# A second level of the seven-product identity in the last block's wide product, and a bias carried as a row of the adapters

## The chip, the cores and the metric

The kernel runs on one core of a Trainium2 chip. The metric is the device time of an execution in microseconds: 261.69 us, the median of three runs (261.42 to 261.91). A core has five engines that run side by side[...]: TensorE (PE: matmuls; PEld: their weight loads), VectorE (DVE), ScalarE (ACT), GpSimd (POOL) and SyncE (SP), whose queue issues nearly all transfers here. Matmuls write into PSUM banks[...].

## The reference, cut to what matters

```python
q_emb = relu(cond @ W3 + b3)                      # (64, 512)
v_sum = sum(v, axis=1, keepdims=True)             # v: (64, 64, 512)
y = relu(((64 * v + v_sum) * q_emb[:, None]) @ W2 + b2)
base = y @ W_base + b_base                        # 512 x 512
shared = (y @ A_s) @ B_s                          # rank 16
gates = softmax(y @ W_router + b_router)          # 6 experts, top 2 kept
routed = sum over e of ((y @ A_r[e]) * w[e]) @ B_r[e]
out = v + base + shared + routed
```

So there are two wide products of 512 by 512 for 4096 tokens, the first with `W2`, the second with `W_base`, all in float32, and between them the gate: the small product `y @ [A_s, A_r, W_router]`, a softmax over six experts, and the two largest kept.

## The kernel before

Everything is held transposed: features on the partitions, tokens along the columns. The tokens go through in four blocks (k = 0 to 3) of 1024, and a block is two column halves (h) of 512. With four chunks of 128 features, a block of y or x is a tile of 128 x (4 chunks, 2 halves, 512).

Both wide products use the seven-product identity of Strassen in Winograd's form. The weight is cut in four quarters of 256 by 256, the block likewise (two feature halves by two column halves); `weight_sums` and `row_sums` build four sums on each side, and seven quarter products (numbered 1 to 7) replace eight. The four row sums in their order are a21 + a22 (the factor of product 5), that minus a11 (of 6), a11 - a21 (of 7), and a12 minus the second (of 3); the factors of 1, 2 and 4 are a11, a12 and a22 themselves. A quarter product is four matmuls of 512 columns (two chunks of depth, two of output). In blocks 1 to 3 the first product applies the identity a second time, inside each of the seven (`first_inner`): each quarter product becomes seven matmuls of 128 x 128 x 256 columns, `q(n, t)`, with n the inner product and t the place in an outer order. The inner products of one t share two banks, "a" and "b", each of two halves (`lo`, `hi`). Between them ScalarE copies a partial result from one half to another (`seed_y`, `seed_z`), and VectorE adds finished parts to the results (`take_1`, `take_21`, `take_22`, `take_u`, `take_w5`; ScalarE copies where nothing is to be added). There are six such banks, so the banks of t come free for t + 3 when the takes of t are done.

The inner identity needs its own sums of sums. For the weights `inner_weight_sums` builds them once (`inner_t`, from `w2_sb` and `t2`, on VectorE). For the rows `prepare_inner` builds them: most on VectorE ahead of time, those of products 2 and 4 on GpSimd inside `first_inner` (L315 to L318: eight subtractions and additions of 256 columns), followed on GpSimd by the e3 and p5 adds (L543, L546), which combine two results, and then ScalarE's bias and relu (L340) into y.

The loop of a block (L758 on): `first_inner` (block 0: `first_mixed`), the loads of the x rows that are added at the end (`load_rows`, into four tiles that the first product has just left), eight groups of small matmuls into `ph` (L779), with the last part of the first product (`rest`) after the second group, the row sums of y on VectorE (L263 to L266), and `second`, which has the gate.

`gate` is a chain of twelve small operations on VectorE with ScalarE's exp among them. Then `hw` weighs the adapters' activations (L683, VectorE), eight transposes turn it round (L704, into `pt`), ScalarE copies it to `hwT`, and GpSimd takes the difference of the two halves, `hwd` (L708). The adapters' second weights `bcat_sb` (112 rows: seven adapters of rank 16) enter as eight more matmuls into the same banks (L641). A result leaves as `with_x` (L637: bank + bias column `bb_sb` + x row, on VectorE) or `leave` (L662), followed by its store. In block 3 the last bank is cut into 384 and 128 columns (`last`, `part`, `last_routed`), whose stores go by two queues, so that the one that ends last is small.

While `second` runs, the preparation of the next block's rows is dealt out in portions (`behind`, `fill`, `share`): the sums over tokens of `modulate` (L206 to L208: scale q, reduce, multiply by q, on VectorE), ScalarE's scaling (L212), the row sums and inner sums. What a portion has not done by then `first_inner` does. All four engines keep the order in which the code issues their instructions; nothing reorders it.

Of the kernel before, what the change touches and what calls it, by code (L numbers as in the profile page):

```python
# [9 lines left out]
F32 = mybir.dt.float32  # L10
AF = mybir.ActivationFunctionType
ALU = mybir.AluOpType
# [20 lines left out]
HC = GR + E  # L33


@with_exitstack
def adaln_ffn(ctx: ExitStack, tc: tile.TileContext, xa, x0, x1, head, w3, w2, wb, a, bcat, br, outT):
# [47 lines left out]
    NH0 = NQ * B + 3 * NC  # L85
    head_sb = const.tile([P, NH0 + NQ * P], F32, tag="head_sb", name="head_sb")
    cond_sb = head_sb[:, : NQ * B].rearrange("p (c b) -> p c b", c=NQ)
    b3_sb, b2_sb, bb_sb = (head_sb[:, NQ * B + n * NC : NQ * B + (n + 1) * NC] for n in range(3))
# [30 lines left out]
    bcat_sb = loaded(bcat, [GR, D], "bcat_sb")  # L119
# [24 lines left out]
    def inner_weight_sums(w, t, name):  # L144

        at = {i: n for n, i in enumerate((5, 6, 7, 4, 1, 2, 3))}
        it = const.tile([P, 4, 7, P], F32, tag=name, name=name)
# [10 lines left out]
        for o, b in groups:  # L158
            i = [it[:, n, o] for n in range(4)]
            steps += [  # L160
                lambda i=i, b=b: nc.vector.tensor_tensor(i[0], b(0, 1), b(0, 0), ALU.subtract),
                lambda i=i, b=b: nc.vector.tensor_tensor(i[1], b(1, 1), i[0], ALU.subtract),
                lambda i=i, b=b: nc.vector.tensor_tensor(i[2], b(1, 1), b(0, 1), ALU.subtract),
                lambda i=i, b=b: nc.vector.tensor_tensor(i[3], b(1, 0), i[1], ALU.subtract),
            ]
# [89 lines left out]
    def row_sums(a, name, cols=slice(0, TB)):  # L255
# [5 lines left out]
        def steps(c=slice(0, KH)):  # L261
# [4 lines left out]
                lambda: nc.vector.tensor_tensor(s[3][:, c], a12[:, c], s[1][:, c], ALU.subtract),  # L266
# [31 lines left out]

    def prepare_inner(k):
# [13 lines left out]
        def steps(g, a, engine=nc.vector):  # L313
            return [
                lambda: engine.tensor_tensor(s[g][:, 0], a(0, 1), a(1, 1), ALU.add),  # L315
                lambda: engine.tensor_tensor(s[g][:, 1], s[g][:, 0], a(0, 0), ALU.subtract),
                lambda: engine.tensor_tensor(s[g][:, 2], a(0, 0), a(0, 1), ALU.subtract),
                lambda: engine.tensor_tensor(s[g][:, 3], a(1, 0), s[g][:, 1], ALU.subtract),  # L318
            ]

# [103 lines left out]
    def first_inner(k, y):  # L424
# [94 lines left out]
        for step in inner[k]["late"]:  # L519
            step()  # L520
        fill(2)
# [52 lines left out]
    def gate(k, ph):  # L574
# [10 lines left out]
        nc.scalar.activation(g, lg, AF.Exp)  # L585
        sm = small.tile([P, 2 * NS], F32, tag="sm", name=f"sm_{k}")
# [29 lines left out]
    def second(k, y, ph, res):  # L616
# [17 lines left out]
        def with_x(name, j, f, h):  # L634

            t = row(f, h)
            nc.vector.scalar_tensor_tensor(t, ps[name, j], bb_sb[:, f : f + 1], t, ALU.add, ALU.add)  # L637
            return t
# [9 lines left out]
        def part(p, cols, i, start):  # L648
            for c in range(KH):
                nc.tensor.matmul(  # L650
                    p[:, cols], tb[i][:, c, ts(1, P)], sy[i][:, c, cols], start=start and c == 0, stop=False,
                    skip_group_check=True,
                )

        def last_routed(p, cols, hw):
            nc.tensor.matmul(
                p[:, cols], bcat_sb[:, ts(KH + 1, P)], hw[:GR, cols], start=False, stop=True,
                skip_group_check=True,
            )

        def leave(p, f, h, add, cols=slice(0, TB), queue=nc.sync):
            nc.vector.tensor_tensor(add[:, cols], p[:, cols], add[:, cols], ALU.add)  # L662
            queue.dma_start(outT[k, f, h, :, cols], add[:, cols])
# [5 lines left out]
        def share():  # L669
# [12 lines left out]
        hw = small.tile([P, 2 * NS, GR], F32, tag="hw", name=f"hw_{k}")  # L682
        nc.vector.tensor_tensor(  # L683
            hw.rearrange("p s (g r) -> p s g r", r=R),
            ph[:, :, :GR].rearrange("p s (g r) -> p s g r", r=R),
            w.unsqueeze(3).to_broadcast([P, 2 * NS, G, R]),
            ALU.mult,
        )
# [12 lines left out]
        pt = ps_h.tile([P, 2 * NS, P], F32, tag="ph", name=f"pt_{k}")  # L701
        hwT = small.tile([P, 2, TB], F32, tag="hwT", name=f"hwT_{k}")
        for s in range(2 * NS):
            nc.tensor.transpose(pt[:GR, s, :], hw[:, s, :], ident)  # L704
        for h in range(2):
            nc.scalar.copy(hwT[:GR, h], pt[:GR, ts(h, NS)].rearrange("p s t -> p (s t)"))  # L706
        hwd = small.tile([P, TB], F32, tag="hwd", name=f"hwd_{k}")
        nc.gpsimd.tensor_tensor(hwd[:GR], hwT[:GR, 0], hwT[:GR, 1], ALU.subtract)  # L708
# [4 lines left out]
        routed("x", 0, 0, hwT[:GR, 0])  # L713
        finish("x", 0, 0, 0)
        routed("z", 0, 0, hwT[:GR, 1])
        finish("z", 0, 0, 1)

        routed("w", 0, KH, hwT[:GR, 1])
        leave(ps["w", 0], KH, 1, u22[0])
        share()  # L720
        if k < NB - 1:
            prod(5, 1, "w")
            routed("w", 1, KH + 1, hwT[:GR, 1])
            leave(ps["w", 1], KH + 1, 1, u22[1])
        else:
            last = [(ps_p.tile([P, TB], F32, tag="pp", name=f"last_{lo}"), slice(lo, hi), queue)
                    for lo, hi, queue in ((0, 3 * P, nc.sync), (3 * P, TB, nc.scalar))]
            for p, cols, queue in last:
                part(p, cols, 5, True)
                last_routed(p, cols, hwT[:, 1])  # L730
                leave(p, KH + 1, 1, u22[1], cols, queue)
# [106 lines left out]
```

## Time and profile before

| | us |
|---|---|
| median of three runs (range) | 261.69 (261.42 to 261.91) |
| the profiled execution | 261.56 |
| its span, first to last instruction | 259.8 |
| TensorE busy | 254.8 (98%) |
| VectorE busy | 193.9 (75%) |
| ScalarE busy | 136.5 (53%) |
| GpSimd busy | 38.7 (15%) |
| block 3: first product | 196.0 to 217.1, and 0.4 after the second group |
| block 3: eight groups of small matmuls | 217.1 to 224.7 |
| block 3: second product with adapters | 224.7 to 256.6 |

The profile gives one execution in us from its first instruction. A row of a timeline has start, duration, engine, line, operation, output <- inputs, sizes, how many are merged, and in brackets the idle time before it and what ended it. In the chain a row is start, duration and what then held up the end. PE's rows count instructions: a float32 matmul is two.

### The profile page before, as it was taken

What the parts mean: (1) busy time and instruction counts of PE and PEld (TensorE: products, weight loads), DVE (VectorE), ACT (ScalarE), POOL (GpSimd) and SP (SyncE); (2) the same over time, 40 slices, a digit from 0 to 9 for tenths busy, and PEclk for the clock granted to TensorE, in tenths of its full rate; (3) what the DMA queues carried; (4) which work ended last, traced back from release to release, by engine and by line L of the source; (5) the groups of instructions that cost most, each with busy time, mean ns of one, the idle gap of its engine ahead of it and who ended that gap; (6) DMA issues with size and microseconds to landing.
All of it is one profiled execution on the core that took longest, in us unless ns stands there. A gap on an engine that the chain in (4) does not pass through costs nothing.

```text
span 259.8 us, 3177 instructions
## 1 busy us (share of the span) xinstructions
PE 254.8 (98%) x1004; PEld 164.5 (63%) x1004; DVE 193.9 (75%) x386; ACT 136.5 (53%) x373; POOL 38.7 (15%) x53
## 2 busy tenths in 40 slices
PE   7999999999999999999999999999999999999995
PEld 3756896454478888444458889544447889745453
DVE  2899898799968967968995894988895475872332
ACT  2399496596048896289017889349404428112000
POOL 1000000020017610002006630002001770000100
PEclk9999999999999999999999999999999999999999
DMA  6997629303320044000521025200332023400233
GB/s 194 360 352 295 261 99 390 156 3 121 121 81 0 11 156 161 0 3 6 196 81 42 0 83 168 76 0 3 121 121 81 0 77 92 159 0 3 76 139 108
DMA packets 14145, 28.54 MB, mean 110 GB/s; under 512 B 1472, under 2 KB 2496, under 8 KB 14128
## 3 DMA queue, kind: packets, MB, share of 16 engines
q1 hardware_dynamic: 13840, 28.21, 30.6%
q8 instruction: 8, 0.13, 0.2%
q10 hardware_dynamic: 288, 0.13, 0.2%
q14 instruction: 9, 0.07, 0.1%
HBM read 19.94 MB, written 8.39 MB: 109 GB/s over the span
## 4 chain that ended last, share of the span: by engine, by line
PE 94%; ACT 2%; DMA 2%; SPq 0%; issue 0%; DVE 0%
PE ia L446 13%; PE ph L779 11%; PE oz L170 11%; PE ox L170 11%; PE ib L446 10%; PE ow L170 9%; PE py L354 5%; PE oy L170 5%; PE ow L641 5%; PE oz L641 3%; PE ox L641 3%; DMA w_sb<-in_w_dram 2%; PE yw L170 1%; PE pt L704 1%; PE last L650 1%; PE yz L170 1%
## 5 line engine op out<-in xcount | busy, mean ns | idle before, releaser
L212 ACT ACTIVATE x<-x,vsum,nq 128x64 f32<-128x64 f32 x192 | 67.5, 431 | 7.0 <-DVE vsum L208 7.0
L779 PE MATMUL ph<-a_sb,y 128*128 128x118 f32 x256 | 30.5, 276 | 0.3 <-ACT y L340 0.3
L779 PEld LDWEIGHTS ph<-a_sb,y 128*128 128x128 f32 x256 | 30.0, 192 | 1.2 <-ACT y L340 0.7
L437 DVE TENSOR_TENSOR u<-ib,u 128x256 f32<-128x256 f32 x42 | 16.4, 419 | 18.5 <-PE ib L446 18.3
L452 ACT COPY ib<-ia 128x256 f32<-128x256 f32 x21 | 7.6, 361 | 42.3 <-PE ia L446 42.3
L170 PE MATMUL ox<-y,wb_sb 128*128 128x512 f32 x64 | 29.5, 593 | 0.0
L708 POOL TENSOR_TENSOR hwd<-hwT 112x512 f32<-112x512 f32 x4 | 5.8, 1452 | 136.1 <-ACT hwT L706 136.1
L170 PEld LDWEIGHTS ox<-y,wb_sb 128*128 128x128 f32 x64 | 11.9, 190 | 13.4 <-issue 13.2
L437 DVE TENSOR_TENSOR u<-ia,u 128x256 f32<-128x256 f32 (+1 forms) x36 | 16.1, 462 | 2.9 <-ACT u L484 1.6
L446 PE MATMUL ib<-inner_s,inner_t 128*128 128x256 f32 x60 | 17.8, 384 | 0.0
L340 ACT ACTIVATE y<-u,head_sb 128x256 f32<-128x256 f32 (+1 forms) x30 | 15.8, 585 | 3.8 <-DVE u L412 3.2
L637 DVE SCALAR_TENSOR_TENSOR xu<-oz,head_sb,xu 128x512 f32<-128x512 f32 x16 | 12.0, 749 | 7.3 <-PE oz L170 4.8
L207 DVE TENSOR_REDUCE vsum<-x 128x8 f32<-128x512 f32 x24 | 16.2, 676 | 0.0
L170 PE MATMUL oz<-sy,tb 128*128 128x512 f32 x32 | 15.2, 599 | 0.0
L170 PE MATMUL oz<-y,tb 128*128 128x512 f32 x32 | 15.1, 593 | 0.0
L170 PE MATMUL oy<-sy,tb 128*128 128x512 f32 x32 | 15.0, 592 | 0.0
L354 PE MATMUL py<-v,w_sb 128*128 128x512 f32 (+1 forms) x40 | 14.4, 510 | 0.7 <-DMA w_sb<-in_w_dram 0.7
L170 PE MATMUL ow<-sy,tb 128*128 128x512 f32 x28 | 13.2, 592 | 0.0
L170 PE MATMUL ow<-sy,wb_sb 128*128 128x512 f32 x28 | 13.2, 592 | 0.0
L455 ACT COPY ib<-ib 128x256 f32<-128x256 f32 x21 | 7.6, 363 | 10.0 <-PE ib L446 10.0
L446 PEld LDWEIGHTS ib<-inner_s,inner_t 128*128 128x128 f32 x60 | 11.2, 190 | 2.2 <-ACT ib L455 0.8
L250 ACT ACTIVATE v<-x,vsum,nq 128x64 f32<-128x64 f32 x32 | 11.0, 427 | 1.7 <-DVE vsum L248 1.7
(173 smaller groups left out, 461.6 us busy)
## 6 DMA issues: line engine op xcount, KB each, us to landing
xu<-in_x_dram SPq DMA_DIRECT2D x16, 512.0 KB, 4.2
out_dram<-xu SPq DMA_DIRECT2D x30, 256.0 KB, 2.0
x<-in_x_dram SPq DMA_DIRECT2D x12, 512.0 KB, 7.5
x<-in_x_dram SPq DMA_DIRECT2D x7, 256.0 KB, 5.7
w_sb<-in_w_dram SPq DMA_DIRECT2D x4, 256.0 KB, 5.5
wb_sb<-in_wb_dram SPq DMA_DIRECT2D x4, 256.0 KB, 4.9
w_sb<-in_w_dram SPq DMA_DIRECT2D x1, 384.0 KB, 4.7
out_dram<-xu SPq DMA_DIRECT2D x2, 192.0 KB, 1.9
```

Source lines behind the costliest of these rows:

```text
L170: nc.tensor.matmul(ps, w[i][:, c, ts(j, P)], s[i][:, c, :], start=start and c == 0, stop=c == KH - 1, skip_group_check=True,)
L207: nc.vector.tensor_reduce(vsum[:, c, bs], xc, AX.XY, ALU.add)
L212: nc.scalar.activation(x, x, AF.Identity, bias=vsum[:, c, b : b + 1], scale=nq[:, c, b : b + 1])
L250: nc.scalar.activation(v[:, c, :, ts(b, NH)], batches_of(c, b, b + 1)[:, :, 0], AF.Identity, bias=vsum[:, c, b : b + 1], scale=nq[:, c, b ...
L340: nc.scalar.activation(y[:, f, h, cols], src, AF.Relu, bias=b2_sb[:, f : f + 1])
L354: nc.tensor.matmul(p[:, :, lo * NH : hi * NH], w2_sb[:, c, ts(f, P)], v[:, c, :, lo * NH : hi * NH], start=(c == 0 and lo == 0), stop=(c = ...
L437: add = lambda o, a, b: nc.vector.tensor_tensor(o, a, b, ALU.add)
L446: nc.tensor.matmul(bank[b, t][:, cols], t_side(o, n), s_side(o, n), start=n == 1, stop=True, skip_group_check=True,)
L452: nc.scalar.copy(bank["b", t][:, lo], bank["a", t][:, lo])
L637: nc.vector.scalar_tensor_tensor(t, ps[name, j], bb_sb[:, f : f + 1], t, ALU.add, ALU.add)
L641: nc.tensor.matmul(ps[name, j], bcat_sb[:, ts(f, P)], hw, start=False, stop=True, skip_group_check=True)
L779: nc.tensor.matmul(ph[:, h * NS + s, :HC], y[:, c, h, ts(s, P)], a_sb[:, c, :], start=(c == 0), stop=(c == NC - 1),)
```

## The change

The diff does two things.

First, block 3's second product also goes through two levels. `second_inner` takes the place of `second` there. Its inner weight sums (`inner_tb`, 28 sums of 128 x 128) are built by GpSimd in two portions inside `first_inner`: four operations of 512 columns in block 2, four of 256 and four of 128 in block 3, both behind the eight of L315 to L318 and ahead of the e3 and p5 adds. Its inner row sums are built between the end of block 3's first product and their use, partly on VectorE (those of factors 1, 4 and 6), partly on GpSimd (2, 7, 5 and 3, and the fourth row sum itself). The first inner products stand among the last two groups of small matmuls; the gate stands at t = 1, with two takes inside it; weighing at t = 2, the transposes at t = 3. Results that several outputs need are passed on by adds on GpSimd, and the outputs leave in pieces of 256 or 512 columns. The cut last bank is gone.

Second, in all blocks `b_base` is no longer a column that VectorE adds but a 113th row of `bcat_sb`, with a column of ones in `hw`, which GpSimd sets (`weigh`); `with_x` becomes a plain add of two operands. A new tile `bcat_d` holds the difference of two column chunks of `bcat_sb` for the inner products; GpSimd builds it once, when `bcat_sb` has landed.

```diff
+GB = GR + 1
...
-    NH0 = NQ * B + 3 * NC
+    NH0 = NQ * B + 2 * NC
...
-    bcat_sb = loaded(bcat, [GR, D], "bcat_sb")
+    bcat_sb = loaded(bcat, [GB, D], "bcat_sb")
...
-    def inner_weight_sums(w, t, name):
+    def inner_weight_sums(w, t, it, engine=nc.vector):
...
         for step in inner[k]["late"]:
             step()
+        if k == 2:
+            all_t = xpool.tile([P, NC, 2, TB], F32, tag="x", name="inner_tb").rearrange("p c h t -> p (c h t)")
+            wide["t"], wide["steps"] = inner_weight_sums(
+                wb_sb, tb, all_t[:, : 28 * P].rearrange("p (n o m) -> p n o m", n=4, o=7), nc.gpsimd
+            )
+        if k > 1:
+            for step in wide["steps"][:4] if k == 2 else wide["steps"][4:]:
+                step()
...
+    def weigh(k, ph):
+        hw = small.tile([P, 2 * NS, GB], F32, tag="hw", name=f"hw_{k}")
+        nc.gpsimd.memset(hw[:, :, GR:], 1.0)
+        nc.vector.tensor_tensor(
...
+    def turn(k, hw):
...
+        for s in range(2 * NS):
+            nc.tensor.transpose(pt[:GB, s, :], hw[:, s, :], ident)
+        for h in range(2):
+            nc.scalar.copy(hwT[:GB, h], pt[:GB, ts(h, NS)].rearrange("p s t -> p (s t)"))
+        return hwT
...
-    def gate(k, ph):
+    def gate(k, ph, between=None):
...
         nc.scalar.activation(g, lg, AF.Exp)
+        if between:
+            between()
...
-            nc.vector.scalar_tensor_tensor(t, ps[name, j], bb_sb[:, f : f + 1], t, ALU.add, ALU.add)
+            nc.vector.tensor_tensor(t, ps[name, j], t, ALU.add)
...
+    def second_inner(k, y, res):
+        order = (1, 2, 6, 7, 5, 4, 3)
...
+        run(sums_of(1, of_y(0, 0)))
+        run(sums_of(2, of_y(KH, 0), nc.gpsimd))
...
+        def row_side():
+            run(sums_of(4, of_y(KH, 1)))
+            got, steps = row_sums(y, "sy")
+            sy.update(got)
+            steps = steps(fourth=nc.gpsimd)
+            of_s = lambda o: lambda c, r: sy[o][:, c, ts(r, R2)]
+            run(steps[:2])
+            run(sums_of(6, of_s(6)))
+            run(steps[2:3])
+            run(sums_of(7, of_s(7), nc.gpsimd))
+            run(sums_of(5, of_s(5), nc.gpsimd))
+            run(steps[3:])
+            run(sums_of(3, of_s(3), nc.gpsimd))
...
+        def first_part():
+            open_banks(0)
+            q(1, 0)
+            q(5, 0)
+            seed_y(0)
+            take_w5(0)
+
+        def second_part():
+            q(6, 0)
+            seed_z(0)
+            take_u(0)
...
+        def main_part(ph):
+            for t in range(1, 7):
+                if t > 1:
+                    take_1(t - 2)
+                open_banks(t)
+                q(1, t)
+                q(5, t)
+                seed_y(t)
+                if t > 1:
+                    q(4, t - 2)
+                    routed(t - 2, 4)
+                    take_21(t - 2)
+                q(7, t - 1)
+                routed(t - 1, 22)
+                if t == 1:
+                    gate(k, ph, lambda: (take_22(0), take_w5(1)))
+                else:
+                    take_22(t - 1)
+                    take_u(t - 1)
+                    take_w5(t)
+                if t == 2:
+                    hw = weigh(k, ph)
+                q(3, t - 1)
+                q(6, t)
+                seed_z(t)
+                q(2, t - 1)
+                routed(t - 1, 1)
+                if t == 3:
+                    hwT = turn(k, hw)
+                    hws["second"] = hwT[:GB, 1]
+                if t == 4:
+                    pr = ps_h.tile([P, 2 * NS, P], F32, tag="ph", name=f"pr_{k}")
...
+                        accumulate(pr[:, j], bcat_sb[:, ts(j, P)], hwT[:GB, 0], True)
+                    add(x12, x12, u)
+                if t == 5:
+                    add(x11, pr, x11)
+                    hws["less"] = difference(k, hwT)[:GB]
+                if t == 6:
+                    add(x11, x11, p1)
+                    leave(0, 0, x11)
+            add(x22, x22, v7, nc.gpsimd)
+            take_1(5)
...
+            add(x22, x22, p5, nc.gpsimd)
+            leave(KH, 1, x22)
+            q(7, 6)
...
+            take_1(6)
+            q(4, 6)
+            routed(6, 4)
+            take_21(6)
...
+    bcat_d = const.tile([GB, KH, P], F32, tag="bcat_d", name="bcat_d")
+    bcat_pairs = bcat_sb.rearrange("p (f j m) -> p f j m", f=KH, j=KH)
+    nc.gpsimd.tensor_tensor(bcat_d, bcat_pairs[:, :, 0], bcat_pairs[:, :, 1], ALU.subtract)
...
+        two = second_inner(k, y, res) if k == NB - 1 else None
         for n, (h, s) in enumerate(groups):
             if rest and n == 2:
                 rest()
+                if two:
+                    two["sums"]()
+            if two and n in two:
+                two[n]()
...
+        if two:
+            two["all"](ph)
+            continue
```

In `two`, place 6 is `first_part`, 7 is `second_part`, "sums" is `row_side`. The helper `inner_row_steps` is the old inner `steps` of `prepare_inner`, taken out: four operations, each `sums_of` runs it once. `routed(t, n)` adds the adapters' matmuls of 256 columns for the outer products 5, 4 and 3, four each; `pr` is their share of the output x11, two of 512 columns.

## The prediction

> **What bounds the kernel now.** I read the page's busy shares and chain first, then the chain in order of time over the last block.
>
> ```profile
> PE 254.8 (98%) x1004; PEld 164.5 (63%) x1004; DVE 193.9 (75%) x386; ACT 136.5 (53%) x373; POOL 38.7 (15%) x53
> PE 94%; ACT 2%; DMA 2%; SPq 0%; issue 0%; DVE 0%
> ...
> 216.26 0.86 PE ia L446 x4
> 217.12 1.78 PE ph L779 x16
> ...
> 238.43 0.87 PE pt L704 x8
> 239.31 1.72 PE oz L170 x4
> ...
> 256.56 0.02 issue
> 256.59 0.29 DVE xu L662
> ```
>
> TensorE runs without a gap, so what it does is the time: a matmul of 512 columns takes 0.86 us (two instructions), one of 256 takes 0.43, exactly half. The last second product runs from 224.69 to 256.56, then one add and a store end the span at 259.8. GpSimd is almost idle, and that is where the change puts work. So I looked for where GpSimd met VectorE: their timelines at 118 us and at 147 us (start and duration in us), VectorE first.
>
> ```profile
> 118.47 0.69 DVE L265 TENSOR_TENSOR s<-x 128x512 f32<-128x512 f32 x1
> 119.07 1.76 DVE L266 TENSOR_TENSOR s<-x,s 128x512 f32<-128x512 f32 x1
> ...
> 147.59 0.43 DVE L206 TENSOR_SCALAR nq<-q_sb 128x16 f32<-128x16 f32 x1
> ...
> 148.64 0.59 DVE L208 TENSOR_TENSOR vsum<-vsum,q_sb 128x8 f32<-128x8 f32 x1
> ...
> 149.87 0.17 DVE L208 TENSOR_TENSOR vsum<-vsum,q_sb 128x8 f32<-128x8 f32 x1
> ```
>
> ```profile
> 118.78 1.50 POOL L708 TENSOR_TENSOR hwd<-hwT 112x512 f32<-112x512 f32 x1 [27.07 <-ACT hwT L706]
> ...
> 146.72 2.49 POOL L543 TENSOR_TENSOR inner_late<-u,u 128x512 f32<-128x512 f32 x2 [2.21 <-DVE u L437]
> ```
>
> L266 takes 1.76 instead of 0.69 us: it ends 0.55 after the GpSimd subtraction (120.28). That one took 1.50 instead of 1.26 because L265 was still running. L208 (0.17 alone) takes 0.59 and ends with the second GpSimd add; L206 ends with the first and slips in between the two. Adds with a PSUM input (L437) keep their 0.42 us beside GpSimd. So VectorE operations with two SBUF inputs and GpSimd operations exclude each other, whole instructions at a time, and they seem to take turns.
>
> **The Trainium skill.** "SBUF — State Buffer", Who interferes with whom: a VectorE instruction with two SBUF inputs contends with a GpSimd instruction that reads SBUF; the later one blocks fully. The lines above agree. "GPSIMD Engine Reference", 3.1: a 2048-column float32 add takes 4.50 us there; with this trace's 1.26 (512 columns) I estimate 2.35 for 1024. "TensorE: Matmul & The Clock Gate", What's actually happening: after an idle window of about 3.4 us the clock halves. No stall here is so long (clock 1.0 throughout), so nothing shows it.
>
> **The change part by part** (the clock of the profile before).
>
> *TensorE's work.* Removed: 28 matmuls of 0.86 = 24.1 and 8 for the adapters = 6.9, with the transposes' 0.87 together the 31.9 from 224.69 to 256.56. Added: 49 of 0.43 = 21.1; adapters 2 of 0.86 and 12 of 0.43 = 6.9; transposes 0.87: 28.9. Gain 3.0 us, if nothing waits. That block 3's first product does 48 of its own 49 in 21.0 us (196.11 to 217.12) speaks for it; but most of its sums were ready beforehand.
>
> *The bias row.* 113 rows for 112 cost no matmul time (rows of 112 and of 128 partitions both show 592 ns); VectorE's add with x falls from 0.75 to 0.69, hidden under TensorE; so are the resets of the extra column in blocks 0 to 2 (0.1 us, GpSimd idle 27 us beforehand). But `bcat_d`, one GpSimd subtraction of 256 columns (0.73), runs when `bcat` lands: by the transfers issued at 13.69, 5.3 to landing, 19.0. VectorE is then in its run of two-SBUF subtractions for `t2`, `inner_t` and `s` (17.96 to 25.8, no gap); its second `s` sum ends at 24.63 and the matmul that needs it starts at 24.77. Blocked 0.56, slack about 0.15: **+0.4**. If it lands elsewhere: 0 to 0.6.
>
> *Block 2.* Four GpSimd sums of 512 columns (1.26, dependent ones 0.1 more: 5.0) go ahead of the e3 adds, which move from 146.72 to 149.5. VectorE's L206 and two L208 now wait for each: the last, at 150.15, ends at 150.78 instead of 150.04. VectorE has no gap from 147.59 to 154.2, and the matmul at 150.75 starts as its operand is written: **+0.75** (0 to 1.2).
>
> *Block 3's first product.* Eight GpSimd sums (4 of 0.73, 4 of about 0.46: 4.7) push the end of the p5 adds from 213.65 to 215.7. The take of product 4's W5 overwrites what they read: VectorE 214.81 becomes 215.7, its matmul (216.09) loses **0.1**, and VectorE enters the last stage 0.4 late.
>
> *The last stage, step by step.* Queues first. GpSimd: sums of factor 2 (4 of 0.73), of 7 (4), of 5 (4), the fourth row sum (2.35), sums of 3 (4), and only then the reset of the ones column that the transposes wait for. VectorE: sums of 1, the last take, sums of 4, the first two row sums, sums of 6, the third row sum, then the gate.
> VectorE's sums of 1 start at 218.2, GpSimd's of 2 at 218.45 (last relu of e3): taking turns, both end near 221.5. The last take, then relu, are 1.8 late, still ahead of their matmuls (223.9). Sums of 4 end at 223.2, two row sums of 1.22 at 225.6, sums of 6 at 227.2, the third at 228.3. The gate started at 225.7 before; now at 228.3.
> At that moment GpSimd, which waits for the third row sum, starts the sums of 7, back to back. Of the gate's operations seven have two SBUF inputs (subtract the maximum, scale, equal, greater, times `tri`, plus, weight), and each waits for one GpSimd sum of about 0.7. Ends: subtraction 229.1, the two takes between 229.8, scale 230.6, equal 231.6, greater 232.5, times `tri` 233.4, plus 234.3, weight 235.0; 4.1 us before (225.72 to 229.85), now 6.7. ScalarE's exp waits for the subtraction (229.4), and behind it the copy that seeds product 2's third bank half (229.7); its matmul stands at 230.0: no loss. Whether the weight or the fourth row sum gets the port at 234.9 is open; if the row sum, the first stall below grows by 2.3, the second shrinks by 1.9.
> Behind it on VectorE stand the takes of product 1 and 2 that free their banks (three of 0.38): 236.1. TensorE, at 0.43 a matmul, reaches the one that needs the bank (the fourth part of product 2) at 232.6: **stall 3.5**.
> TensorE is at the transposes at 238.3. GpSimd: the fourth row sum from 235.0 to 237.3, sums of 3 to 240.25, reset 240.4: **stall 2.15**.
> From 240.4: transposes 0.87, 26 matmuls 11.2, adapters 6.9: 259.4. The x rows' last load waits for the last relu (222.4), lands by 227 at the row's 4.5, and is read after 243. The later waits have slack by the same count (the difference `hwd` ready at 251, needed at 256.4; x22's last GpSimd add at 258.2, ahead of the last store). Net of the stage: 259.4 − 256.56 = **+2.8**.
>
> *The end.* The last add is 256 columns (0.42 for 0.29), its store 128 KB for 64, behind 768 KB issued in the 2 us before it: **+0.4** (0.2 to 0.8).
>
> Sum: 0.4 + 0.75 + 2.8 + 0.4 = +4.35 (block 3's 0.1 is in the 2.8). Profiled execution 261.56 (span 259.8 and 1.8 around it) + 4.35 = 265.9; the runs' median is 0.13 above the profiled one, within their spread, so I leave it: **265.9**.
>
> **Rivals.**
> *Turns cost nothing* (the overlap at 118 us is a special case, or GpSimd and VectorE rarely meet): the early 0.4 and block 2's 0.75 vanish, the gate ends by 232. The reset still stands behind 13 GpSimd operations: from 227.1, 12 of about 0.72 and one of 2.35, 238.3, while TensorE is there at 234.8. Stall 3.5 against a gain of 3.0, +0.1, +0.4: +1.0, **262.6**. Against it: four blocked instructions in the trace.
> *No turns: GpSimd keeps the port* through its queue. The gate's seven wait for its gaps, some end after 240; the transposes then wait for the gate, not the reset: +2 to +4 more, **269**. L206 between two adds speaks against it.
> *The clock.* The stall of 3.5 lies at the edge of the skill's 3.4; a half clock for one window costs up to 1.7: **267.6**.
> *Faster.* GpSimd finishes before TensorE arrives: it decides at the transposes, if the reset is done by 234.8 and the bank by 232.6. From 228.3, 13 operations would have 6.5 us, 0.5 each on average; the 256-column row shows 0.73. Then only the gain and the end count: −2.6, **259.0**. The same holds if GpSimd's sums start 4 us earlier, for which the third row sum would have to be ready at 224.
> *The adapters or stores bind:* the stores are the same 2 MB, and DMA is busy 16% from 225 to 257; no.
>
> **How the numbers follow.** My forecast with turns 0.60 (its own range 264.3 to 267.3, from the bounds above); turns free 0.16; clock 0.12; port kept 0.08; faster 0.04. Below 262.6 lies the last and half of the first rival; above 268.3 the kept port: 262.6 to 268.3 holds 8 in 10. A change within 0.2% (0.5 us, about what a measurement can tell from none) asks for the turns free and the GpSimd queue 0.6 us shorter: 0.04. Slower 0.92.
>
> **What would show it.** TensorE: two gaps between 228 and 241, the first ended by VectorE, the second, before `pt`, by GpSimd's reset; no other above 0.3 in the last stage. VectorE: gate operations of 0.2 and 0.46 stretched to 0.7 to 1.1, reduces not. GpSimd: the sums of 7, 5 and 3 nearly back to back. Early: one VectorE subtraction near 19.3 lengthened by 0.56; in block 2, L208 lengthened and 0.75 more from the first product's start to `ph`. The last product's 49 matmuls still at 0.43. I am wrong if the transposes wait for nothing, if the two gaps together are below 3, or if small VectorE operations keep their lengths beside GpSimd.

## The result, and the profile after

The changed kernel takes 274.52 us (median of four runs, 273.62 to 275.31) against 261.56 (261.41 to 261.91) before: ratio 1.0493, 95% interval 1.0465 to 1.0521. The prediction was 265.9 with a range of 262.6 to 268.3. The direction was right and the size was not: of 13 us lost it had foreseen a little over 4. (Two of the four executions of the 113-row load below, the profiled one among them, lie more than 1.5% above the fastest; they count as slow runs and are left out of its ratio.)

The page of the changed kernel: busy time of TensorE and the other engines, the granted clock by slices, and the chain's shares by engine.

```profile
PE 255.4 (94%) x1046; PEld 174.1 (64%) x1046; DVE 208.8 (77%) x417; ACT 142.2 (52%) x391; POOL 74.6 (27%) x95
...
PEclk9999989999999999999999999999999999999997
...
PE 71%; DMA 10%; DVE 7%; POOL 6%; ACT 2%; issue 1%; SPq 1%; POOLq 0%; DVEq 0%
```

Where the chain before was 94% TensorE and 2% DMA, 10% of it is now DMA, some 27 us of a 272 us span, and the prediction let no load of data cost anything. The chain in order of time says which transfers these are; two loads of x make up 20.7 us of them (start, duration, what):

```profile
9.29 5.42 DMA x<-in_x_dram
...
14.73 15.26 DMA x<-in_x_dram
29.99 0.02 issue
30.01 0.70 DVE vsum L207
...
31.82 1.13 PE yw L170 x4
```

A load of `x_1`, issued at 14.73, lands at 29.99. VectorE sits idle 3.59 us for it, and TensorE, behind VectorE, 3.71 us until 31.82, in block 0, which the change hardly touches. Behind the wait TensorE is also slow:

```profile
31.82 1.13 PE L170 MATMUL yw<-s,w_sb 128*128 128x256 f32 x4 [3.71 <-DVE u L411]
...
34.18 1.91 PE L170 MATMUL yy<-s,t 128*128 128x256 f32 x4
```

Four such instructions took 1.03 us in the kernel before. The clock granted to TensorE, 1.00 at full speed, is 0.77 at 32 to 34 us, 0.50 at 34 to 36 and 0.87 at 36 to 38 (it is the 8 in the row above); in the kernel before it is 1.00 all through. The work from this matmul to the first `ph` takes 7.84 us instead of 6.14.

The last stage, TensorE's timeline (start, duration, operation, in brackets the idle time and what ended it):

```profile
239.22 0.59 PE L813 MATMUL ja<-inner_sy,inner_tb 128*128 128x256 f32 x2
243.04 0.70 PE L813 MATMUL jb<-y,inner_tb 128*128 128x256 f32 x2 [3.22 <-DVE xu L770]
...
244.87 0.59 PE L813 MATMUL ja<-sy,tb 128*128 128x256 f32 x2
247.28 1.13 PE L599 MATMUL pt<-ident,hw 128*113 128x128 f32 x8 [1.81 <-POOL hw L586]
```

and the gate on VectorE, then two of GpSimd's sums from the same microseconds:

```profile
235.59 0.55 DVE L618 TENSOR_TENSOR lg<-lg,mx 128x48 f32<-128x48 f32 x1
...
237.66 0.90 DVE L635 TENSOR_TENSOR eq<-g 128x288 f32<-128x288 f32 x1
238.49 0.97 DVE L636 TENSOR_TENSOR gt<-g 128x288 f32<-128x288 f32 x1
...
241.29 0.45 DVE L640 TENSOR_REDUCE rank<-gt 128x48 f32<-128x288 f32 x1
```

```profile
237.53 0.72 POOL L304 TENSOR_TENSOR inner_sy<-sy,inner_sy 128x256 f32<-128x256 f32 x1
238.22 0.93 POOL L301 TENSOR_TENSOR inner_sy<-sy 128x256 f32<-128x256 f32 x1
```

These are the two gaps that the prediction drew: the first (3.22 us) ended by a take on VectorE behind the gate, the second (1.81) by GpSimd's reset of the ones column. The four comparisons, with two SBUF inputs, take 0.86 to 0.97 us instead of 0.45; the reduce keeps its length.

A ledger shows where the time went. Four points are in both traces: VectorE's first gate operation of block 0 (it follows the first `ph`), the first `ph` matmul of block 3, the end of TensorE, the end of the span. All numbers are us from the span's start; the middle rows are differences of these.

| | before | after | difference |
|---|---|---|---|
| gate of block 0 starts | 41.11 | 46.99 | +5.9 |
| from there to `ph` of block 3 | 175.85 | 176.79 | +0.9 |
| from there to TensorE's end (256.56, 266.61) | 39.60 | 42.83 | +3.2 |
| from there to the end of the span | 3.24 | 5.09 | +1.9 |
| span | 259.8 | 271.7 | +11.9 |

The first row is not all the load's. In the eleven profiled runs whose loads are not 113 rows (below, and the kernel before) the gate of block 0 starts anywhere from 40.9 to 43.0 us; in the two that load 113 rows at once it starts at 47.0 and 48.2. In this trace 0.5 of the 5.9 us is there before the wait, the wait is 3.7, and 1.7 comes from the low clock behind it.

The three other executions of the changed kernel have spans of 272.3, 273.4 and 273.0 us at lower mean clocks (0.986, 0.977 and 0.981 for 0.988), so the median time is 0.9 us longer than the one that this trace explains.

### The profile page after: what moved, and what is told of

Its sections match the earlier page's. It is cut to its first block, busy times and chain, and to the rows that moved or that the text cites. A ratio compares the mean times of both kernels' runs of the same rounds, so it can differ in the third digit from the quotient of the medians.

```text
span 271.7 us, 3375 instructions
## 1 busy us (share of the span) xinstructions
PE 255.4 (94%) x1046; PEld 174.1 (64%) x1046; DVE 208.8 (77%) x417; ACT 142.2 (52%) x391; POOL 74.6 (27%) x95
## 4 chain that ended last, share of the span: by engine, by line
PE 71%; DMA 10%; DVE 7%; POOL 6%; ACT 2%; issue 1%; SPq 1%; POOLq 0%; DVEq 0%
PE ia L447 10%; PE ph L1001 8%; PE oz L170 8%; DMA x<-in_x_dram 8%; PE ox L170 8%; PE ow L170 8%; PE ib L447 8%; PE ow L678 4%; PE oy L170 4%; PE ja L813 3%; PE jb L813 3%; DMA w_sb<-in_w_dram 2%; PE ox L678 2%; PE oz L678 2%; DVE u L438 2%; PE pt L599 1%
## 5 line engine op out<-in xcount | busy, mean ns | idle before, releaser
L453 ACT COPY ib<-ia 128x256 f32<-128x256 f32 x21 | 7.6, 360 | 42.8 <-PE ia L447 42.8
L606 POOL TENSOR_TENSOR hwd<-hwT 113x512 f32<-113x512 f32 x4 | 5.6, 1393 | 86.5 <-ACT hwT L601 86.5
L170 PE MATMUL ox<-y,wb_sb 128*128 128x512 f32 x48 | 22.1, 593 | 0.0
L301 POOL TENSOR_TENSOR inner_two<-x 128x256 f32<-128x256 f32 x3 | 2.2, 725 | 55.9 <-PE ib L447 55.9
L170 PEld LDWEIGHTS ox<-y,wb_sb 128*128 128x128 f32 x48 | 8.9, 190 | 10.0 <-issue 9.8
L770 POOL TENSOR_TENSOR xu<-xu,parts 128x256 f32<-128x256 f32 (+2 forms) x8 | 11.0, 1378 | 6.6 <-DVE parts L770 6.5
L170 PE MATMUL oz<-sy,tb 128*128 128x512 f32 x24 | 11.5, 601 | 0.0
L355 PEld LDWEIGHTS py<-v,w_sb 128*128 128x128 f32 x40 | 7.4, 190 | 6.3 <-issue 4.5
L170 PE MATMUL oz<-y,tb 128*128 128x512 f32 x24 | 11.3, 592 | 0.0
L170 PE MATMUL ow<-sy,tb 128*128 128x512 f32 x24 | 11.3, 592 | 0.0
## 6 DMA issues: line engine op xcount, KB each, us to landing
x<-in_x_dram SPq DMA_DIRECT2D x12, 512.0 KB, 12.6
```

What stands on the lines that cost most here:

```text
L170: nc.tensor.matmul(ps, w[i][:, c, ts(j, P)], s[i][:, c, :], start=start and c == 0, stop=c == KH - 1, skip_group_check=True,)
L355: nc.tensor.matmul(p[:, :, lo * NH : hi * NH], w2_sb[:, c, ts(f, P)], v[:, c, :, lo * NH : hi * NH], start=(c == 0 and lo == 0), stop=(c = ...
L770: add = lambda o, a, b, engine=nc.vector: engine.tensor_tensor(o, a, b, ALU.add)
```

## The experiments

"Load in two" below means the changed kernel with the adapters' weights loaded as 112 rows and one row. The later experiments start from it.

### The load alone: 113, 128 and 118 rows in the kernel before

```diff
-    bcat_sb = loaded(bcat, [GR, D], "bcat_sb")
+    bcat_sb = loaded(bcat, [113, D], "bcat_sb")[:GR]    # and 128, and 118; rows of zeros added
```

> The kernel before with one thing changed: the adapters' second weights are loaded as 113 rows (the last row zeros, used by nothing) in the one transfer. Theory A, the load itself is the early loss: its data stand in few of the DMA engines, it lands near 29 us instead of 19, x_1's loads behind it land late, VectorE waits some 3.6 us for x_1 and TensorE some 3.7 us at 28 to 32 us; whole run 266 to 268 us. Theory B, the early loss comes from the difference of the weights on GpSimd or from another order of the issues: this run stays at 261.6 (within 0.5).

> The kernel before with the adapters' second weights loaded as 128 rows (16 rows of zeros, used by nothing). Theory A with the number 113 as the cause (it divides among the DMA engines badly): lands near 19 us as in the kernel before, 261.4 to 261.9. If instead any load longer than 112 rows is slow: like the run with 113 rows, 266 or more.

> The kernel before with the adapters' second weights loaded as 118 rows (six rows of zeros, used by nothing). Theory A in its sharp form, that a load is split over the greatest number up to 16 that divides its rows (113: 1 engine; 128 and 112: 16): 118 rows go over 2 engines, land some 7 us later than with 16 engines less what one engine costs, between 21 and 25 us, and x_1 is late by part of it: 262 to 264.5. If every row count that 16 doesn't divide goes over one engine: 267 to 269 as with 113 rows. If only odd or prime counts are bad: 261.4 to 262.

Measured: 268.14 us with 113 rows (264.18 to 269.17, ratio 1.0163, interval 1.0081 to 1.0245); 261.79 with 128 (ratio 0.9999, 0.9983 to 1.0016); 261.65 with 118 (ratio 1.0003, 0.9986 to 1.0019). One row of zeros that nothing reads brings the early loss by itself: in the profiled execution the gate of block 0 starts at 48.22 (41.11 before), VectorE waits 3.86 us for `x_1` and TensorE 3.98, and the clock is 0.50 from 32 to 36 us. What it costs scatters, from 2.5 to 7.5 us over the 261.7 of the kernel before, and the mean clocks of the four executions scatter with it (0.993 in the fastest, 0.986 and 0.987 in the two longest). Sixteen rows of zeros cost nothing, so it is the number 113 and not the length.

How the number works is seen in the DMA view from 13 to 40 us, in 40 slices of 0.675 us: the busy share of the core's 16 DMA engines in tenths, and what they moved. First 113 rows, then 118, then the kernel before with 112.

```profile
DMA  9999951197999999988999997979110000000000
GB/s 379 355 368 388 373 222 49 39 146 297 416 391 322 334 309 331 319 264 300 373 334 346 319 370 297 140 267 376 55 36 24 30 24 24 24 30 24 18 0 0
```

```profile
DMA  9999999999999984969999998211110000259999
GB/s 357 349 379 398 388 367 309 291 279 285 297 346 285 285 243 188 134 182 364 407 455 395 407 455 364 73 79 55 55 42 24 0 0 0 79 194 358 364 416 361
```

```profile
DMA  9999999999999991539999999200000000129999
GB/s 385 352 364 388 385 346 270 303 316 425 425 395 401 407 370 49 73 79 388 431 394 425 443 407 394 79 12 18 0 0 0 0 0 0 39 97 340 306 398 404
```

With 113 rows the loads end in a tail of some six us at 18 to 36 GB/s, most of it at 24 to 30, a busy share that rounds to 0 tenths of 16. That looks like one engine that still has work when fifteen are done; the view doesn't show single engines. With 118 rows the tail is shorter and moves 42 to 79 GB/s, two or three times as much. With 112 there is a scrap of it. The Trainium skill says so outright ("DMA: Bandwidth & Descriptors", Why a DMA increments its semaphore by 16 and not by 1): a transfer goes over the largest number of engines, at most 16, that divides its slowest dimension; it gives 127 rows as a case of one engine. 113 is a prime (one engine), 118 is 2 times 59 (two), 112 and 128 go over 16. The tails agree with one and two. At 24 to 30 GB/s the 226 KB take one engine 7.7 to 9.6 us (an estimate from the tail's rate). If a sixteenth of every other load also goes through that engine, as the rule has it for 128 rows, `x_1` and `x_2`, issued next, wait behind it; the 512 KB loads of x from 14 to 45 us do land later, after 12.9 us in the median with 113 rows, 9.2 with 118 and 7.5 with 112. With 118 rows VectorE takes `x_1` up at 25.67 us, as before, and waits for nothing. So the expectation of 262 to 264.5 for 118 rows was missed because the slack of `x_1` covered the delay. The time alone, 261.65, is what the other theory (only odd or prime counts are bad) expected; the tail and the landing times are what speaks for two engines.

### The load in two transfers

```diff
-    bcat_sb = loaded(bcat, [GB, D], "bcat_sb")
+    bcat_sb = const.tile([GB, D], F32, tag="bcat_sb", name="bcat_sb")
+    nc.sync.dma_start(bcat_sb[:GR], bcat[:GR])
+    nc.sync.dma_start(bcat_sb[GR:], bcat[GR:])
```

> The changed kernel with the adapters' second weights loaded as two transfers, 112 rows and then the one bias row. Theory A: the 112 rows land near 19.5 us, the one row soon after, the early loss of 5.5 to 5.9 us goes: 268 to 269.5, and what is left over the kernel before (block 2 +0.7, block 3 +0.25, last stage +3.2, end +1.9) stays, about 267.6 to 269. Theory B: no gain, 274 to 275.

268.48 us (268.05 to 269.63), ratio 1.0269 (1.0237 to 1.0300): 6.0 us of the 13 are back. The 112 rows land 5.4 us after their issue, VectorE and TensorE have no wait at 25 to 32 us, the clock there is 1.00, and GpSimd starts the difference of the weights when the prediction had it:

```profile
19.09 0.73 POOL L968 TENSOR_TENSOR bcat_d<-bcat_sb 113x256 f32<-113x256 f32 x1 [17.37 <-DMA bcat_sb<-in_bcat_dram]
```

Beside it one small VectorE operation takes 0.23 us instead of 0.16, and nothing else is longer: a reduce was running, and it kept its 0.68 us. The gate of block 0 starts at 43.02, within the spread of the runs without the 113-row load. The rest of the ledger stays as it was: 176.8, 42.8 and 5.2 us.

### The bias row alone

The kernel before with the 113th row (in two transfers), the ones column, and the plain add with x; its last block's second product stays on one level.

```diff
-            nc.vector.scalar_tensor_tensor(t, ps[name, j], bb_sb[:, f : f + 1], t, ALU.add, ALU.add)
+            nc.vector.tensor_tensor(t, ps[name, j], t, ALU.add)
...
-        hw = small.tile([P, 2 * NS, GR], F32, tag="hw", name=f"hw_{k}")
+        hw = small.tile([P, 2 * NS, GB], F32, tag="hw", name=f"hw_{k}")
+        nc.gpsimd.memset(hw[:, :, GR:], 1.0)
```

> The bias row alone, loaded as 112 rows and one: the kernel before with the bias as the 113th row, its last block's second product on one level as before. If the row costs only its load: 261.4 to 262.2. If the ones column and 113-row operands cost something by themselves: 0.5 us or more above 261.6.

261.41 us, ratio 0.9995 (0.9978 to 1.0013). The row as such costs nothing and brings nothing; only its load was dear.

### GpSimd's sums of the weights, moved

```diff
-        if k > 1:
-            for step in wide["steps"][:4] if k == 2 else wide["steps"][4:]:
-                step()
...
         hwd = difference(k, hwT)
+        if k == 2:
+            ...
+            for step in wide["steps"]:
+                step()
```

> The changed kernel with the load in two transfers (268.48), and all twelve sums of the second weights on GpSimd moved from the first products of blocks 2 and 3 to block 2's second product, behind the difference of the weighted rows. Theory A (the prediction's steps 3 and 4): TensorE's wait of 0.66 us in block 2's first product goes, and so do some 0.2 us in block 3's: 267.4 to 267.9. Theory B, the sums cost as much in their new place, where they take turns with VectorE's work for block 3: 268.3 to 269.

267.08 us (266.36 to 268.72), ratio 1.0191 (1.0129 to 1.0254), against 268.48 for the load in two, and 0.3 below the expected range. In the changed kernel the wait looks like this:

```profile
157.33 0.70 PE L447 MATMUL ia<-x,t 128*128 128x256 f32 x2 [0.66 <-DVE u L438]
```

Here it is gone, and from the gate of block 0 to `ph` of block 3 it takes 175.7 us instead of 176.8, as in the kernel before (175.85). The 0.9 of that row of the ledger belongs to these sums. The times of this run scatter more than that, so it is the trace that shows it here. The twelve sums cost nothing visible in their new place.

### The reset ahead of the sums

```diff
+        early_hw = hw_tile(k)          # allocates hw and resets its last column on GpSimd
         run(sums_of(1, of_y(0, 0)))
...
-                    hw = weigh(k, ph)
+                    hw = weigh(k, ph, early_hw)
```

> The changed kernel with the load in two transfers (268.48), and the last block's reset of the ones column issued ahead of all of GpSimd's sums of that block. Theory A (the prediction's step 5): the second stall, 1.81 us in the changed kernel and 0.41 in the run with the load in two, goes; the weights from VectorE are ready at 240.3 and TensorE comes at 241.3 (full clock) to 242.4 (lowered clock): 266.6 to 268.1. Theory B, a wait takes its place at once, since the sums on GpSimd that the third to seventh product need end no earlier: 268.3 to 268.7.

267.63 us (266.63 to 268.50), ratio 1.0207 (1.0162 to 1.0253). TensorE's timeline in the last stage has the first gap and no second one:

```profile
238.20 0.70 PE L820 MATMUL jb<-y,inner_tb 128*128 128x256 f32 x2 [3.22 <-DVE xu L776]
...
240.46 1.04 PE L605 MATMUL pt<-ident,hw 128*113 128x128 f32 x8
```

From `ph` to TensorE's end it takes 40.7 us instead of 42.8. No other wait takes its place.

### The sums held until the gate has ended

```diff
+            def later():
+                nc.gpsimd.tensor_copy(mark, w[:, 0, 1:2])      # waits for the gate
+                run(sums_of(7, of_s(7), nc.gpsimd))
+                run(sums_of(5, of_s(5), nc.gpsimd))
+                run(steps[3:])
+                run(sums_of(3, of_s(3), nc.gpsimd))
...
                     hw = weigh(k, ph)
+                    later()
```

> The changed kernel with the load in two transfers (268.48), and in the last block the sums of 7, of 5, the fourth row sum and the sums of 3 on GpSimd held back until the gate has ended (a one-column copy of the gate's result on GpSimd ahead of them); the reset of the ones column is then ahead of them too. Theory A, the gate is long because GpSimd's sums and its small operations with two inputs take turns: the four comparisons of the gate take 0.45 us each again instead of 0.86 to 0.98, the gate with its two adds some 4.9 us instead of 6.9, the first stall some 1.3 us instead of 3.2, the second gone: 264.5 to 266.2. Theory B, the gate is long for itself or the sums are late then (TensorE waits for the sums of 7, 5 or 3): 268 or more.

264.85 us (264.38 to 265.00), ratio 1.0099 (1.0063 to 1.0136). VectorE's timeline, the same comparisons alone:

```profile
230.41 0.21 DVE L620 TENSOR_TENSOR lg<-lg,mx 128x48 f32<-128x48 f32 x1
...
231.91 0.46 DVE L637 TENSOR_TENSOR eq<-g 128x288 f32<-128x288 f32 x1
232.28 0.45 DVE L638 TENSOR_TENSOR gt<-g 128x288 f32<-128x288 f32 x1
```

The gate with its two takes runs from 229.94 to 234.33, 4.4 us instead of 6.9, and `ph` to TensorE's end is 38.6 us: 4.2 less than in the changed kernel, 1.0 less than in the kernel before. One gap is left, in another place: TensorE waits 1.44 us for the first of the held sums of 7. The end grew instead, to 6.0 us, since GpSimd, later with everything, ends its last adds of x22 after TensorE.

### The end

```diff
-            add(x22, x22, v7, nc.gpsimd)
+            add(x22, x22, v7)
...
-            add(x22, x22, p5, nc.gpsimd)
+            add(x22, x22, p5)
```

> The changed kernel with the load in two transfers (268.48) and one more edit: the two adds of x22 that end its sums run on VectorE instead of GpSimd. Theory A, the end grew because GpSimd's four adds (7.6 us) hold x22 back and stretch x11's last add on VectorE (2.70 us), so that 1.8 MB of stores leave in one heap in the last 6 us: the stores of x11 and x22 leave 1.5 to 4 us earlier, from TensorE's end to the span's end 3.3 to 3.7 us instead of 5.2, whole run 266.5 to 267.2. Theory B, the end is set by the bytes that the last product leaves whatever the order: 268.3 to 268.8.

267.62 us (267.25 to 267.66), ratio 1.0205 (1.0169 to 1.0241): 0.9 less, outside what was expected. The DMA view from 235 us to the end of the changed kernel (40 slices of 0.925 us) shows the heap of stores that this was about, with GpSimd's last four adds behind it:

```profile
DMA  0000000000000000000000000000300099999900
GB/s 0 0 0 0 0 0 0 0 0 0 0 18 0 0 0 0 0 0 0 0 0 0 0 0 0 0 0 0 136 6 0 0 334 359 341 374 360 337 21 0
```

```profile
258.42 7.62 POOL L770 TENSOR_TENSOR xu<-xu,parts 128x512 f32<-128x512 f32 x4 [0.54 <-DVE parts L770]
```

Of 2.1 MB of stores all but one of 256 KB leave within the last 8 us and fill the DMA for six slices, 2 to 3 us beyond the last issue (267.19). With x22 on VectorE the stretch from TensorE's end to the span's end fell from 5.2 to 3.5 us, as expected, but only in part because the stores left earlier. TensorE also ended later: from `ph` to its end it took 44.5 us instead of 42.8. Counted from the first `pr` matmul, behind which the clock is full in both runs, to the end of the span it is 19.6 us instead of 20.5, the 0.9 of the times. VectorE's adds now stood ahead of a take that TensorE waited for:

```profile
261.31 0.70 PE L815 MATMUL jb<-sy,inner_tb 128*128 128x256 f32 x2 [0.55 <-DVE xu L772]
```

and the clock was low after the first gap. Here are two windows of the same run: bounds and length in us; busy us and number of instructions of TensorE, its weight loads, VectorE, ScalarE and GpSimd; then the granted clock, DMA share and GB/s.

```profile
235.00:238.00 3.00, 0.81 (x2) 0.72 (x3) 2.93 (x8) 0.36 (x1) 3.00 (x3) 0.74 0.00 0
238.00:240.00 2.00, 2.00 (x6) 1.55 (x6) 2.00 (x6) 0.00 (x0) 1.84 (x4) 0.50 0.03 8
```

### All repairs together

The load in two, the weights' sums in block 2's second product, the held sums, and the end in a better order: x11's add of product 1 in the fourth part, where VectorE has a gap, and x22's two adds on VectorE in the last part, ahead of the takes that the seventh product needs.

```diff
+                if t == 4:
+                    add(x11, x11, p1)
+                if t == 6:
+                    add(x22, x22, v7)
...
                     add(x11, pr, x11)
+                    leave(0, 0, x11)
...
-                    add(x11, x11, p1)
-                    leave(0, 0, x11)
-            add(x22, x22, v7, nc.gpsimd)
+                    add(x22, x22, p5)
+                    leave(KH, 1, x22)
...
-            add(x22, x22, p5, nc.gpsimd)
-            leave(KH, 1, x22)
```

> The changed kernel with four repairs together: the load in two transfers; the twelve sums of the second weights in block 2's second product; the GpSimd sums of 7, 5, the fourth row sum and 3 held until the gate has ended; x11's add of product 1 moved to its fourth part, and x22's two adds on VectorE in the last parts, so that both leave early. If the causes add up: from the run with the held sums (264.85) less 0.9 for block 2 and 3, less 1.3 to 1.9 for the end: 261.5 to 262.7, the same as the kernel before or up to 0.3 per cent from it. If the last stage then finds another wait (VectorE late for the last takes, as in the run with x22 on VectorE alone, 0.55 us): 262.7 to 263.5. Below 261.2 the change would be worth its name.

260.74 us (260.49 to 261.24), ratio 0.9962 (0.9948 to 0.9976): 0.4% faster than the kernel before, by 1.0 us, with an interval clear of 1, and better than expected. Its ledger: gate of block 0 at 41.45, then 175.7 us to `ph`, 38.4 to TensorE's end (before 39.6), 3.5 to the end of the span (before 3.2). The repair of the end was worth more here than alone: holding the sums had made the end 6.0 us long, and it is 3.5 here with TensorE's stage all but the same (38.6 and 38.4). This pair of runs shows what the order of the last adds costs better than the run above. One gap is left, and the clock stays at 1.00 behind it:

```profile
233.64 0.70 PE L821 MATMUL ja<-inner_sy,inner_tb 128*128 128x256 f32 x2 [1.39 <-POOL inner_sy L303]
```

### The gate spread over the takes

The same repairs, but the gate's comparisons are placed behind the takes of two parts, the transposes and the first routed product one part later, and GpSimd's sums run free.

```diff
-                    hw = weigh(k, ph)
-                    later()
+                    run(held[:2])       # equal, greater
+                if t == 3:
+                    run(held[2:])       # times tri, plus, rank, weight
+                    hw = weigh(k, ph, early_hw)
-                if t == 3:
+                if t == 4:
                     hwT = turn(k, hw)
```

> The same repairs, but the gate's six last operations (four comparisons, rank, weights) don't stand ahead of VectorE's takes: two of them come behind the takes of the third part, four and the weighing behind those of the fourth, the transposes and the first routed product one part later; GpSimd's sums aren't held, and the reset of the ones column comes ahead of them. If the gate in front of the takes is what stalls TensorE: the first stall (1.44 us with held sums, 3.22 without) goes, 260 to 261.5, faster than the run with held sums by 0.5 to 1.5. If VectorE is short in total over these parts, the wait comes back at the transposes or at a take: 262 to 264.

263.18 us (262.92 to 263.40), ratio 1.0055 (1.0043 to 1.0068): slower than holding. The first gap is gone, and the wait comes back at the transposes, where TensorE waits for the weighing:

```profile
240.84 1.13 PE L597 MATMUL pt<-ident,hw 128*113 128x128 f32 x8 [1.94 <-DVE hw L585]
...
243.63 0.70 PE L826 MATMUL jb<-sy,inner_tb 128*128 128x256 f32 x2 [0.80 <-DVE parts L782]
```

The delay stands earlier on VectorE: the third comparison ran beside GpSimd's fourth row sum (235.37 to 237.72) and took 2.05 us instead of 0.45.

```profile
235.98 2.05 DVE L637 TENSOR_TENSOR eq<-eq,tri 128x288 f32<-128x288 f32 x1
```

## Why the prediction was wrong, point by point

**The bias row: the step that failed.** "But `bcat_d` ... runs when `bcat` lands: by the transfers issued at 13.69, 5.3 to landing, 19.0." The 5.3 us were read from a row for 112 rows and carried over to 113. The load of 113 rows took 14.9 us: GpSimd waited for it until 28.94, and `x_1`, issued behind it, reached VectorE at 29.99. The cost was 6.0 us in the times (from the load in two) in place of +0.4; in the trace it is a wait of 3.7 us on TensorE and 1.7 of low clock behind it. The prediction reckoned with the row's matmul, its add and the resets of blocks 0 to 2, all of which were free as it said (592 ns at 112 and 113 rows; row alone 0.9995). It didn't ask how the row's transfer is divided or what stands behind it in the queue, and no rival had a slow load in it. The +0.4 itself was too high: with the load in two, the difference ran at 19.09 as predicted and cost one VectorE operation 0.07 us. That the load alone does it is shown by the 113 rows that nothing reads; that it goes over one engine is read from the tail of the DMA view and from the page's rule.

**How far this explains the miss.** The measured time lies 8.6 us above the forecast. The early part is 5.5 of it, the end 1.5, the last stage 0.4, blocks 2 and 3 some 0.1, and 0.9 is the median's distance from the profiled execution.

**TensorE's work: right.** The last product's instructions ran at 0.43 and 0.86 us. The stage from `ph` grew by 3.2 us. Its gaps, counted from one start to the next, are 0.4, 3.4 and 2.0; the slower first matmuls behind them add some 0.3, which makes 6.1. So the work alone shrank by 2.9 us (3.0 predicted).

**Block 2 and block 3: right.** The prediction had +0.75 and +0.1; 0.9 was measured for both together, and it went when the sums moved. Block 2's wait on TensorE is 0.66 us, ended by VectorE as predicted.

**The last stage: right in its mechanism, +3.2 for +2.8.** The gate took 6.9 us for 6.7 predicted. The first gap was 3.22 for 3.5, ended by the take behind the gate; the second was 1.81 for 2.15, ended by the reset. Operations with two SBUF inputs were stretched; the reduces and the adds with a PSUM input were not. Holding the sums removed the first gap and moving the reset removed the second. Two details differ: there was a short wait ahead of the first gap (0.25 us) that the prediction hadn't drawn, and the seventh of the operations that it counted, the weight, went ahead of the fourth row sum and kept its 0.21 us, a case that it had left open. The rival in which GpSimd's turns cost nothing falls with the held sums (the gate 4.4 us without them, 6.9 with). The one in which GpSimd keeps the port falls too: the comparisons got in between the sums.

**The clock: a rival that was half right, at another wait than the one forecast.** The prediction put it at the first stall of the last stage. In the changed kernel's trace the clock fell at the early wait instead, and that cost 1.7 us, the size that the rival had named. At the gap of 3.22 us, which stands ahead of the same matmuls in five profiled executions, the clock stayed at 1.00 in two (the changed kernel, the reset ahead). In three (load in two, `x22` on VectorE, the weights' sums moved) it was 0.50 for 3, 6 and 6 us behind the gap, and pairs of matmuls took up to 1.06 us. Part of that loss hides in the second gap, which then shrinks (0.41 us in the run with the load in two). Waits of 3.71 and 3.98 us lowered the clock, waits of 1.94 us and less did not. The Trainium skill ("TensorE: Matmul & The Clock Gate", What's actually happening) gives about 3.4 us of idle time; here 3.22 was enough in three executions of five, so it is no sharp limit. The low clock is thus part of the early loss and of the spread of the times, and not the cause of the two gaps.

**The end: the right mechanism was missing.** "+0.4 (0.2 to 0.8)" was reckoned from the last add and the last store; +1.9 was measured. GpSimd's four last adds (7.62 us in all) hold x22 back to 266.04, and x11's last add on VectorE, beside them, takes 2.70 us instead of 1.22. So 1.8 MB leave in one heap, and the DMA works on it for 2 to 3 us beyond the last issue; the prediction had counted 768 KB ahead of the last store. With these adds in another order and on VectorE the end fell from 6.0 to 3.5 us in the runs with held sums, and the run with x22 alone on VectorE was 0.9 us faster. How much of it is x22's and how much x11's was not measured apart.

## What to carry to other kernels

When an edit adds one row to a tensor, cost its transfer anew: here 112 rows landed after 5.3 us and 113 after 14.9, the loads queued behind them came late, and TensorE lost time twice, by the wait and by the low clock after it. A second transfer for the one row cost nothing. Work put on an idle GpSimd wasn't free for VectorE: ask which VectorE operations with two SBUF inputs run in the same microseconds, and hold the GpSimd work until they are through if TensorE waits for them. Read the end by the stores that are still to be written when TensorE stops, not by the last instruction alone.

## What was not expected of the hardware

- One row more made a load land after 14.9 us instead of 5.3, and the 512 KB loads of x from 14 to 45 us after 12.6 in the median instead of 7.5. Sixteen rows more changed nothing; six rows more were seen in the DMA's tail and not in the time.
- The time of the whole repair is not the sum of single ones: the last adds' place was worth 0.9 us alone and about 2.5 in the profiled executions where the held sums had made the end longer (6.0 us to 3.5).
- A VectorE comparison of 288 columns took 0.45 us alone, 0.9 beside GpSimd sums of 256 columns (0.72), and 2.05 beside one of 1024 (2.35): the longer the GpSimd instruction it met, the larger the loss. The last is one instance.
